# Sending six of eight head groups through the output projection with seven half-size products, summed by accumulating DMAs

## The chip, the cores and the metric

The kernel runs on one core of a Trainium2 chip. The metric is the device time in microseconds of one execution, here the median of three runs. All data are float32.

## The reference

One transformer block on `x` of 2 batches x 512 tokens x 512 features, with 32 heads of 128. Cut to what matters:

```python
q, k, v = rms_norm(n @ Wq + bq, gq), rms_norm(n @ Wk + bk, gk), n @ Wv + bv     # n = layernorm(x)
p = softmax(q_h @ k_h.T / sqrt(128))                                            # for each batch and head h
o_h = p @ v_h
attn = concat(o_h) @ Wo + bo                                                    # Wo: 4096 x 512
x = x + layernorm(attn)
x = x + layernorm(ffn(layernorm(x)))                                            # a linear layer and gated low-rank experts
```

## The kernel before, in words

The kernel does four stages one after the other: the projection to q, the projection to k, the attention loop (with the values' projection woven in), and the tail (residual, feed-forward, output).

**Projections.** `project` (L174) goes over 8 groups of 4 heads. It already uses a seven-product form: with batches as one pair and feature halves as the other, seven products of half size and some sums replace eight products. The sums of weights are made by GpSimd (`weight_sums` L163, `value_sums` L287), those of tokens by VectorE (`token_sums` L150). q, k and v are kept in DRAM and fetched again in the loop (`fetch`, `fetch_v`).

**The attention loop (L533)** has 64 iterations `i`, one per head and batch (`h, b = divmod(i, 2)`); eight iterations are one group `g` of 4 heads. The engines' order is that of the program (`IN_ORDER`: TensorE, VectorE, ScalarE, GpSimd; SyncE's DMA queue, SP, is not in that set). In iteration `i`:

- VectorE: `sums(i-1)` (L459 `quarters`, L467 `part`: the softmax's denominators), `below_top(i)` (L484, subtracts the maximum), after psd `inv`, `r` and `divided(i-1)` (L475 to L502), `top_of(i+1)` (L450, L451 `m`), then exits of value products and the addition `y` (L515).
- TensorE: `scores(i+1)` (L440 `pss`), a short matmul `psd` (L473), value products (L384 `v`), one output-projection task `psy` (L514), `weighted(i)` (L496 `o`).
- ScalarE: the scores' exits (L441), the exponential (L487), the value bias (L503).
- GpSimd: one partition maximum (L453 `top`), for which `below_top` of the next iteration waits.

**The output projection.** In group `g`'s iterations the tasks `outward(g-1, n)`, n from 0 to 7, run, one per iteration. Each has 4 matmuls: for one tile of 128 tokens, the group's four heads times their 128 x 512 rows of Wo, into one bank of PSUM. VectorE then adds the bank to the running sum `ys[n]` in SBUF. The eighth group's tasks come after the loop.

**Values.** 28 of their 112 tile steps come before the loop, 28 in its first 8 iterations, the rest until iteration 43. From iteration 44 on the loop has no value products.

**Buffers.** PSUM has two sets of 4 banks: `ps` for scores and psd, `aux` for the values, psy and o. A float32 matmul of the program is two records in the trace.

## Time and profile before

| | |
|---|---|
| median of 3 runs | 1365.17 us (1364.51 to 1367.77) |
| the profiled execution's own time | 1363.96 us |
| its span, first to last instruction | 1362.2 us |
| mean granted TensorE clock | 0.988 |
| DMA | 214.75 MB, mean 158 GB/s |

How to read the profile: PE is TensorE's matmul, PEld its weight load, DVE is VectorE, ACT ScalarE, POOL GpSimd, SPq the queue from which SyncE issues DMAs. A group row has line, engine, operation, output<-input, shapes and count, then busy time and the mean of one in ns, then the idle time just before and what ended it. In a row of windows stand the stretch, its length, the busy time of PE, PEld, DVE, ACT and POOL with the number of records in brackets, the granted clock, the DMA share and GB/s. A row of the timeline or of the chain has start, duration (us), engine and line.

```profile
POOL 3478888565763011111111111111111111111000
PEclk9999999999998999999999999999999999999988
DMA  6486665599999865532343252352343131300101
```

These are three of the rows with 40 equal slices of the span in tenths: GpSimd's busy share, the granted clock, the DMA engines' busy share. GpSimd is busy in the q and k projections (the first 12 or so slices), and little in the loop.

### The profile page before, as it was taken

Reading aid. Unit: us, or ns where it says so; the run is one execution under the profiler, and the core shown is the slowest. Engines: PE = TensorE matmul, PEld = TensorE weight load, DVE = VectorE, ACT = ScalarE, POOL = GpSimd, SP = SyncE. Lnnn points to the kernel's source line nnn. Section 1 sums busy time; section 2 is a strip of 40 time slices with the busy share of each in tenths; the row PEclk is TensorE's granted clock in tenths of the full one; section 3 lists DMA queues with packets and bytes.
Section 4 is the critical chain, followed back from the end, with each engine's and each line's share of the span. In section 5 each row is a group of like instructions: output and inputs, shape, how many; then the busy total and the mean of one; then the engine's idle time right before and its main releaser. Section 6 shows DMA issues by size and latency. Waiting matters only on the chain.

```text
span 1362.2 us, 10840 instructions
## 1 busy us (share of the span) xinstructions
PE 1319.9 (97%) x3244; PEld 599.4 (44%) x3244; DVE 926.2 (68%) x1206; ACT 488.0 (36%) x655; POOL 400.9 (29%) x294
## 2 busy tenths in 40 slices
PE   4999999999999999999999999999999999999976
PEld 2444444444444444444444444444444444444443
DVE  6443434777754478877777777777677888888566
ACT  4123232222131153443434334343433455444333
POOL 3478888565763011111111111111111111111000
PEclk9999999999998999999999999999999999999988
DMA  6486665599999865532343252352343131300101
GB/s 218 170 282 220 219 221 201 178 314 337 320 323 311 262 208 161 177 132 85 123 155 103 91 188 62 99 171 91 108 147 101 62 123 55 116 31 24 55 0 62
DMA packets 115083, 214.75 MB, mean 158 GB/s; under 512 B 10192, under 2 KB 10832, under 8 KB 115024
## 3 DMA queue, kind: packets, MB, share of 16 engines
q1 hardware_dynamic: 115024, 214.05, 47.0%
q8 instruction: 26, 0.43, 0.1%
q14 instruction: 33, 0.27, 0.1%
HBM read 136.42 MB, written 77.59 MB: 157 GB/s over the span
## 4 chain that ended last, share of the span: by engine, by line
PE 68%; DVE 2%; DMA 1%; ACT 0%; issue 0%; ACTq 0%
PE pss L440 16%; PE o L496 16%; PE psy L514 16%; PE v L384 14%; PE f L626 2%; PE p_k L192 2%; PE f L676 1%; PE psd L473 1%; PE hg L618 1%; DMA w_v<-keptw 1%; PE nt_f L139 0%; DVE st_z L123 0%; DVE quarters L459 0%; DVE s L484 0%; DVE z L600 0%; ACT s L487 0%
## 5 line engine op out<-in xcount | busy, mean ns | idle before, releaser
L441 ACT ACTIVATE s<-pss,rk 128x512 f32<-128x512 f32 x256 | 175.9, 687 | 464.6 <-PE pss L440 457.8
L453 POOL PARTITION_ALL_REDUCE top<-m x64 | 114.1, 1783 | 717.1 <-DVE m L451 717.1
L514 PE MATMUL psy<-wo,oh 128*128 128x512 f32 x512 | 230.8, 596 | 0.0
L496 PE MATMUL o<-s,v 128*128 128x512 f32 x512 | 230.3, 592 | 0.3 <-ACT s L487 0.3
L440 PE MATMUL pss<-qh,kh 128*128 128x512 f32 x512 | 230.2, 592 | 0.0
L496 PEld LDWEIGHTS o<-s,v 128*128 128x128 f32 x512 | 97.2, 190 | 123.1 <-issue 121.5
L440 PEld LDWEIGHTS pss<-qh,kh 128*128 128x128 f32 x512 | 97.3, 190 | 122.5 <-issue 122.5
L459 DVE TRANSPOSE_TENSOR_REDUCE quarters<-s 128x64 f32<-128x2048 f32 x64 | 147.3, 2301 | 0.0
L484 DVE TENSOR_TENSOR s<-s,top 128x2048 f32<-128x2048 f32 x64 | 146.0, 2281 | 0.0
L514 PEld LDWEIGHTS psy<-wo,oh 128*128 128x128 f32 x512 | 95.7, 190 | 112.4 <-issue 111.9
L487 ACT ACTIVATE s<-s 128x2048 f32<-128x2048 f32 x64 | 121.7, 1901 | 6.1 <-DVE s L484 6.1
L384 PE MATMUL v<-w_v,t 128*128 128x512 f32 x256 | 120.0, 613 | 3.3 <-DMA w_v<-keptw 3.3
L213 POOL TENSOR_TENSOR accq<-accq,sq_q 128x512 f32<-128x512 f32 x62 | 78.6, 1268 | 55.6 <-ACT sq_q L212 54.5
L213 POOL TENSOR_TENSOR acck<-acck,sq_k 128x512 f32<-128x512 f32 x62 | 85.4, 1382 | 24.7 <-ACT sq_k L212 21.7
L192 PE MATMUL p_q<-t,s_q 128*128 128x512 f32 x192 | 87.8, 607 | 2.6 <-DVE t L158 2.6
L384 PE MATMUL v<-w_v,nT_a 128*128 128x512 f32 x192 | 88.3, 601 | 0.0
L212 ACT ACTIVATE sq_k<-k 128x512 f32<-128x512 f32 x62 | 38.7, 630 | 137.8 <-DVE k L244 67.8
L212 ACT ACTIVATE sq_q<-q 128x512 f32<-128x512 f32 x62 | 39.1, 631 | 133.8 <-DVE q L244 78.2
L192 PE MATMUL p_k<-t,s_k 128*128 128x512 f32 x192 | 85.0, 592 | 0.0
L475 DVE RECIPROCAL inv<-psd 128x16 f32<-128x16 f32 x64 | 16.5, 257 | 99.6 <-PE psd L473 99.6
L450 DVE TENSOR_TENSOR m<-s 128x1024 f32<-128x1024 f32 x64 | 77.8, 1216 | 4.7 <-ACT s L441 4.7
L515 DVE TENSOR_TENSOR y<-psy,y 128x512 f32<-128x512 f32 x56 | 38.4, 691 | 57.6 <-PE psy L514 57.6
(152 smaller groups left out, 1418.5 us busy)
## 6 DMA issues: line engine op xcount, KB each, us to landing
keptq<-q SPq DMA_DIRECT2D x64, 256.0 KB, 4.0
q<-keptq SPq DMA_DIRECT2D x16, 1024.0 KB, 6.5
w_v<-keptw SPq DMA_DIRECT2D x32, 512.0 KB, 4.0
keptk<-k SPq DMA_DIRECT2D x64, 256.0 KB, 6.9
keptqs<-q SPq DMA_DIRECT2D x64, 256.0 KB, 6.9
qh<-keptqs SPq DMA_DIRECT2D x64, 256.0 KB, 2.9
kh<-keptk SPq DMA_DIRECT2D x64, 256.0 KB, 2.7
keptv<-o_v SPq DMA_DIRECT2D x64, 256.0 KB, 3.4
```

What stands on the lines that cost most here:

```text
L192: nc.tensor.matmul(ps, a[:, c, ts(j, P)], x[c], start=(c == 0), stop=(c == 1))
L212: nc.scalar.activation(sq, o, AF.Square)
L213: nc.gpsimd.tensor_tensor(accs[b], accs[b], sq, ALU.add)
L384: nc.tensor.matmul(ps, x[c][:, ts(t, P)], w[:, c, :], start=(c == 0), stop=(c == 1))
L440: nc.tensor.matmul(ps, kk[i][:, ts(k, P)], qs[i], start=True, stop=True)
L441: nc.scalar.activation(s[:, k, :], ps, AF.Copy, scale=rks[b][:, k : k + 1])
L453: nc.gpsimd.partition_all_reduce(ms[i], m[:, 0, :], P, ReduceOp.max)
L459: nc.vector.tensor_reduce(quarters.rearrange("p k j -> p (k j)"), ss[i].rearrange("p k (j r) -> p (k j) r", r=32), AX.X, ALU.add, apply_tr ...
L484: nc.vector.tensor_tensor(s, s, top.unsqueeze(1).to_broadcast([P, NT, 512]), ALU.subtract)
L487: nc.scalar.activation(ss[i], ss[i], AF.Exp)
L496: nc.tensor.matmul(po, vs[b, g, k][:, ts(j, P)], ss[i][:, k, :], start=(k == 0), stop=(k == NT - 1))
L514: nc.tensor.matmul(ps, o[:, ts(t, P)], wos[g][:, j, :], start=(j == 0), stop=(j == GH - 1))
```

## The change

The output projection of groups 0 to 5 is done by seven products. The left side is the heads' outputs, seen as 2 x 2 blocks: batch by even or odd pair member of the heads. The right side is Wo's rows for those heads by the two halves (256 columns) of the output.

- In the q stage SP loads the Wo rows of a group, VectorE makes four sums in place (`output_sums`), SP stores them in DRAM (`keptwo`).
- In every fourth iteration (`n4 == 0`) VectorE makes four sums of heads' outputs (`head_sums`) after `top_of`.
- `through_wo` is one task: a product `i`, a token half `u`, 4 matmuls of 256 columns into one bank. 14 tasks per group are spread over 8 iterations: 2, 2, 2, 1, 2, 2, 2, 1. The right sides are loaded by `load_right`, two products to a tile, at n = 7, 2 and 4.
- The result of a task goes to one of 14 running sums `acc`. For group 0 it is written there directly (VectorE with the bias for products 1 and 5, else ScalarE). For groups 1 to 5 ScalarE copies the bank into SBUF and GpSimd issues a DMA that adds the copy to the running sum.
- When iteration 56 is reached, VectorE makes the output's tiles from the running sums (`combined`, 14 operations, three per iteration). Groups 6 and 7 go the old way: group 6 in the last eight iterations, with each addition held back by an iteration, group 7 after the loop.
- Buffers are regrouped: x and value tiles in larger tiles, 16 `o` tiles for 13, a new pool `gpool`; the last Wo groups come into `hpool` by halves; the running sums take the weights' pool and six `y` tiles.

```diff
...
-    xpool = ctx.enter_context(tc.tile_pool(name="xpool", bufs=B * NT))
+    xpool = ctx.enter_context(tc.tile_pool(name="xpool", bufs=B * NT // 2))
-    ypool = ctx.enter_context(tc.tile_pool(name="ypool", bufs=B * NT))
+    ypool = ctx.enter_context(tc.tile_pool(name="ypool", bufs=6))
-    vpool = ctx.enter_context(tc.tile_pool(name="vpool", bufs=3 * NT))
+    vpool = ctx.enter_context(tc.tile_pool(name="vpool", bufs=4))
-    opool = ctx.enter_context(tc.tile_pool(name="opool", bufs=GH * B + 5))
+    opool = ctx.enter_context(tc.tile_pool(name="opool", bufs=16))
+    gpool = ctx.enter_context(tc.tile_pool(name="gpool", bufs=2))
-        xt = xpool.tile([P, D], F32, tag="x", name=f"{name}{b}_{t}")
+        halves = [xpool.tile([P, 2, D], F32, tag="x", name=f"{name}{b}_{u}") for u in range(NT // 2)]
...
-        out = [vpool.tile([P, 2, 256], F32, tag="v", name=f"s{i + 1}_{name}") for i in range(4)]
-        s1, s2, s3, s4 = out
+        pairs = [vpool.tile([P, 4, 256], F32, tag="v", name=f"s{i}_{name}") for i in range(2)]
+        s1, s2, s3, s4 = out = [t[:, i : i + 2] for t in pairs for i in (0, 2)]
...
+        WG = NG - 2
+        keptwo = dram.tile([WG, 2, P, 2, 512], F32, tag="wo", name="keptwo")
+        woq = wo.rearrange("(g j k p) f -> g k p j f", j=2, k=2, p=P)
+        wo_halves = {}
+        def load_halves(g):
+            pool, tag = ((hpool, "h"), (gpool, "g"))[g % 2]
+            wo_halves[g] = [pool.tile([P, 2, 512], F32, tag=tag, name=f"wo{g}_{k}") for k in range(2)]
+            for k in range(2):
+                nc.sync.dma_start(out=wo_halves[g][k], in_=woq[g, k])
+        def output_sums(g):
+            of = wo_halves[g]
+            (b11, b12), (b21, b22) = ([w[:, :, ts(e, 256)] for e in range(2)] for w in of)
+            nc.vector.tensor_tensor(b11, b12, b11, ALU.subtract)
+            nc.vector.tensor_tensor(b12, b22, b12, ALU.subtract)
+            nc.vector.tensor_tensor(b22, b22, b11, ALU.subtract)
+            nc.vector.tensor_tensor(b21, b22, b21, ALU.subtract)
+            for k in range(2):
+                nc.sync.dma_start(out=keptwo[g, k], in_=of[k])
...
             value_sums(g // 2, g % 2)
+            if 0 < g <= WG:
+                output_sums(g - 1)
+            if g < WG:
+                load_halves(g)
...
-            wos[g] = load_w(wo[ts(g, GH * P), :], f"wo{g}")
+            wos[g] = []
+            for k in range(2):
+                w = hpool.tile([P, 2, 512], F32, tag="h", name=f"wo{g}_{k}")
+                nc.sync.dma_start(out=w, in_=wo[ts(2 * g + k, 2 * P), :].rearrange("(j p) f -> p j f", p=P))
+                wos[g] += [w[:, j, :] for j in range(2)]
...
-        def fetch_v(b, g):
-            for t in range(NT):
-                v = vpool.tile([P, 512], F32, tag="v", name=f"v{b}_{g}_{t}")
-                nc.sync.dma_start(out=v, in_=keptv[b, g, t])
-                vs[b, g, t] = v
+        def fetch_v(b, c):
+            v = vpool.tile([P, NT, 256], F32, tag="v", name=f"v{b}_{c}")
+            src = keptv[b, c // 2].rearrange("t p f -> p t f")
+            nc.sync.dma_start(out=v, in_=src[:, :, ts(c % 2, 256)])
+            vs[b, c] = v
...
+            if (b, h % 2) != (1, 0):
+                left_of[{(0, 0): 1, (0, 1): 2, (1, 1): 4}[b, h % 2], h // 2] = o
+        two_halves = [wpool.tile([P, 4, 512], F32, tag="w", name=f"acc{n}") for n in range(2)]
+        accs = [t[:, n, :] for t in two_halves for n in range(4)]
+        accs += [ypool.tile([P, 512], F32, tag="y", name=f"acc_y{n}") for n in range(6)]
+        accs = [a.rearrange("p (t e) -> p t e", t=2) for a in accs]
+        acc = {i + 1: accs[2 * i : 2 * i + 2] for i in range(7)}
+        right_of = {}
+        def head_sums(c):
+            def tile_of(i):
+                return opool.tile([P, 512], F32, tag="o", name=f"s{i}_o{c}")
+            a11, a12, a21, a22 = (os[b, 2 * c + k] for b in range(B) for k in range(2))
+            s3, s2, s4 = tile_of(3), tile_of(2), tile_of(4)
+            nc.vector.tensor_tensor(s3, a11, a21, ALU.subtract)
+            nc.vector.tensor_tensor(a21, a21, a22, ALU.add)
+            nc.vector.tensor_tensor(s2, a21, a11, ALU.subtract)
+            nc.vector.tensor_tensor(s4, a12, s2, ALU.subtract)
+            left_of.update({(3, c): s4, (5, c): a21, (6, c): s2, (7, c): s3})
+        product_order = (1, 2, 4, 5, 7, 6, 3)
+        def load_right(g, n):
+            w = gpool.tile([P, 2, 512], F32, tag="g", name=f"wr{g}_{n}")
+            for half, i in enumerate(product_order[2 * n : 2 * n + 2]):
+                k, e = {1: (0, 0), 2: (1, 0), 3: (1, 1), 4: (1, 0), 5: (0, 0), 6: (1, 1), 7: (0, 1)}[i]
+                src = (woq if i <= 3 else keptwo)[g, k]
+                nc.sync.dma_start(out=w[:, half, :].rearrange("p (j f) -> p j f", j=2), in_=src[:, :, ts(e, 256)])
+                right_of[i, g] = w[:, half, :].rearrange("p (j f) -> p j f", j=2)
+        def through_wo(g, i, u):
+            ps = pt(f"psw{i}_{g}_{u}", "aux").rearrange("p (t e) -> p t e", t=2)
+            for t in range(2):
+                for j in range(2):
+                    a = left_of[i, 2 * g + j][:, ts(2 * u + t, P)]
+                    nc.tensor.matmul(ps[:, t, :], a, right_of[i, g][:, j, :], start=(j == 0), stop=(j == 1))
+            to = acc[i][u]
+            def add():
+                if g > 0:
+                    new = upool.tile([P, 512], F32, tag="u", name=f"w{i}_{g}_{u}").rearrange("p (t e) -> p t e", t=2)
+                    nc.scalar.copy(new, ps)
+                    nc.gpsimd.dma_start(out=to, in_=new, accum_op=ALU.add)
+                elif i in bias_of:
+                    nc.vector.tensor_tensor(to, ps, bias_of[i].unsqueeze(1).to_broadcast([P, 2, 256]), ALU.add)
+                else:
+                    nc.scalar.copy(to, ps)
+            return add
+        bias_of = {1: bo_b[:, 0:256], 5: bo_b[:, 256:512]}
+        nc.vector.tensor_tensor(bias_of[5], bias_of[5], bias_of[1], ALU.subtract)
+        y_pairs = {}
+        def combined(u):
+            for b in range(B):
+                y_pairs[b, u] = xpool.tile([P, 2, 512], F32, tag="x", name=f"y{b}_{u}")
+            a1, a2, a3, a4, a5, a6, a7 = (acc[i + 1][u] for i in range(7))
+            (c11, c12), (c21, c22) = ([y_pairs[b, u][:, :, ts(e, 256)] for e in range(2)] for b in range(B))
+            for out, p, q, op in (
+                (c11, a1, a2, ALU.add),
+                (a6, a1, a6, ALU.add),
+                (a7, a6, a7, ALU.add),
+                (a6, a6, a5, ALU.add),
+                (c12, a6, a3, ALU.add),
+                (c21, a7, a4, ALU.subtract),
+                (c22, a7, a5, ALU.add),
+            ):
+                yield lambda out=out, p=p, q=q, op=op: nc.vector.tensor_tensor(out, p, q, op)
+        def y_tile(b, t):
+            return y_pairs[b, t // 2][:, t % 2, :]
+        def outward(g, b, t, tag=None):
             ps = pt(f"psy{b}_{g}_{t}", tag or "aux")
             for j in range(GH):
                 o = os[b, g * GH + j]
-                nc.tensor.matmul(ps, o[:, ts(t, P)], wos[g][:, j, :], start=(j == 0), stop=(j == GH - 1))
-            return lambda: nc.vector.tensor_tensor(ys[n], ps, bo_b if g == 0 else ys[n], ALU.add)
-
+                nc.tensor.matmul(ps, o[:, ts(t, P)], wos[g][j], start=(j == 0), stop=(j == GH - 1))
+            return lambda: nc.vector.tensor_tensor(y_tile(b, t), ps, y_tile(b, t), ALU.add)
+        wo_tasks = {i: [] for i in range(N)}
+        for g in range(WG):
+            for k in range(14):
+                wo_tasks[G * (g + 1) + k * G // 14].append(
+                    lambda g=g, k=k: through_wo(g, product_order[k // 2], k % 2)
+                )
+        last = N - G
+        for b, t, n in [(b, t, n) for n, (b, t) in enumerate((b, 2 * u + t) for u in range(2) for b in range(B) for t in range(2))]:
+            wo_tasks[last + n].append(lambda b=b, t=t: outward(WG, b, t))
...
         for i in range(N):
             g, n = divmod(i, G)
             if i + 3 < N:
                 fetch(i + 3)
-            if n == 2:
+            c, n4 = divmod(i, 2 * B)
+            if 2 <= n4 and 0 < c < H // 2 - 1:
+                fetch_v(n4 - 2, c + 1)
+            if g >= WG and n == 6:
                 load_wo(g)
-            if n >= G - 2 and g + 1 < NG:
-                fetch_v(n - G + 2, g + 1)
+            if g < WG and n == 7:
+                for k in range(2):
+                    load_right(g, k)
+            if 0 < g <= WG and n in (2, 4):
+                load_right(g - 1, 1 + n // 2)
+            if n == 0 and g > WG:
+                combining = [step for u in range(2) for step in combined(u)]
             part = sums(i - 1) if i > 0 else None
             below_top(i)
             if i + 1 < N:
@@ -550,29 +680,38 @@
             while left and 84 - left < want:
                 exits.append(next(v_steps))
                 left -= 1
-            adds = [outward(g - 1, n)] if g > 0 else []
+            adds = [task() for task in wo_tasks[i]]
             top_of(i + 1)
+            if n4 == 0 and 0 < c <= 2 * WG:
+                head_sums(c - 1)
+            for _ in range(3):
+                if combining:
+                    combining.pop(0)()
+            if i >= last:
+                held, adds = adds, held
             for work in exits + adds:
                 work()
             po = weighted(i)
+        for add in held:
+            add()
...
-        adds = [outward(NG - 1, n, "ps") for n in range(NT)]
+        adds = [outward(NG - 1, 0, t, "ps") for t in range(NT)]
         for add in adds:
             add()
-        adds = [outward(NG - 1, NT + n, "aux") for n in range(NT)]
+        adds = [outward(NG - 1, 1, t, "aux") for t in range(NT)]
         for b in range(B):
-            x2 = ys[b * NT : (b + 1) * NT]
+            x2 = [y_tile(b, t) for t in range(NT)]
...
```

## The prediction

> **What bounds the kernel now.** I read the page first, then the windows by stage, one iteration of the attention loop in the timeline, the chain of waits, and the rows nearest to the new instructions. Engines on the page:
>
> ```profile
> PE 1319.9 (97%) x3244; PEld 599.4 (44%) x3244; DVE 926.2 (68%) x1206; ACT 488.0 (36%) x655; POOL 400.9 (29%) x294
> ```
>
> TensorE is busy 97% of the span. By stage (Q projection; K projection; loop with values still to do; loop without), TensorE's busy time stands first after the stretch, VectorE's third:
>
> ```profile
> 30.00:235.00 205.00, 202.06 (x470) 89.68 (x469) 84.67 (x126) 53.72 (x84) 154.69 (x124) 0.98 0.64 218
> 235.00:420.00 185.00, 184.41 (x431) 81.48 (x430) 136.30 (x174) 47.05 (x77) 115.31 (x85) 1.00 0.84 288
> 583.00:1058.00 475.00, 475.00 (x1162) 214.80 (x1161) 352.36 (x381) 189.42 (x224) 64.16 (x36) 1.00 0.36 117
> 1058.00:1265.00 207.00, 206.73 (x512) 93.66 (x511) 173.38 (x178) 100.50 (x116) 33.87 (x19) 1.00 0.22 71
> ```
>
> In the loop nothing makes TensorE wait: what leaves its stream leaves the kernel's time, if VectorE, 84% busy in the last stretch, keeps up. One iteration there, from the timeline (in brackets the idle time before and what ended it):
>
> ```profile
> 1181.08 2.30 DVE L459 TRANSPOSE_TENSOR_REDUCE quarters<-s 128x64 f32<-128x2048 f32 x1
> ...
> 1183.60 2.28 DVE L484 TENSOR_TENSOR s<-s,top 128x2048 f32<-128x2048 f32 x1
> ...
> 1187.14 0.29 PE L473 MATMUL psd<-part,same 128*128 128x16 f32 x2
> ...
> 1187.47 0.26 DVE L475 RECIPROCAL inv<-psd 128x16 f32<-128x16 f32 x1 [1.59 <-PE psd L473]
> ...
> 1190.37 0.69 DVE L451 TENSOR_TENSOR m<-m 128x512 f32<-128x512 f32 x1
> ...
> 1191.22 1.78 POOL L453 PARTITION_ALL_REDUCE top<-m  x1 [8.74 <-DVE m L451]
> ```
>
> The next quarters starts at 1191.61, so the period is 10.53 us. VectorE's reserve is the 1.59 us in which it waits for psd; GpSimd is idle 8.74 us.
>
> **TensorE, the gain.** The chain has a Wo task, and the narrowest matmuls with a new weight each, as:
>
> ```profile
> 1187.43 3.53 PE psy L514 x8
> ...
> 1328.91 3.76 PE hg L618 x32
> ```
>
> Each program matmul is two records. Eight in a row take 3.43 us behind a full-width matmul, 429 ns a record of 512 columns (3.53 directly behind the short psd; that 0.1 stays in both kernels). hg has 137 columns and takes 3.76 / 32 = 117.5 ns. On the line between, 256 columns take 117.5 + 119 x 311.5 / 375 = 216 ns. A group of four heads now costs 8 tasks x 3.43 = 27.44 us. Seven products x 2 token halves x 4 matmuls x 2 records = 112 records x 216 = 24.2 us. Six groups: 6 x 3.24 = **19.4 us gained**.
>
> A rule speaks against this. The Trainium skill, "TensorE: Matmul & The Clock Gate", Part 3, says that a weight load overlaps running matmuls only when its row group differs; all of ours use all rows. The LDWEIGHTS row says 190 ns, so by the rule a record costs 216 + 190 = 406 ns, a group 45.5 us, and six groups lose 108 us. The rows contradict it: hg's loads also take 189 ns each, yet its records come every 117.5 ns, so loads do overlap. I take 216; bounds 214.5 (half of 429) and 222.
>
> **VectorE.** Removed: 48 additions of psy at 0.69 us = 33 us. Added in the loop: 12 x 4 head sums like L451 (0.69 us, both inputs in SBUF) = 33 us; 14 combinations = 9.7 us; 4 bias additions = 2.8 us. The total barely moves; what counts is where it falls.
> - Head sums come four at once (about 2.5 us at their pitch) in every fourth iteration. Count from psd's end: m done +3.6, head sums +6.1, quarters and part +8.6, subtraction +10.9, exponential (1.9) done +13.0 with the hand-over. The next weighted matmul starts at +10.5 + 3.5 = +14.0. It fits by about 1 us. Over eight iterations TensorE needs 8 x 7.0 + 24.2 + 0.8 = 81 us, VectorE 8 x (8.94 - 0.61) + 5 = 72. Cost nothing; without this reserve the whole 2.5 us would show every fourth iteration.
> - The combinations add 3 x 0.62 in iterations 56 to 60, where psy additions remain: 8.94 + 1.9 = 10.8 against 10.53, five times, 1.4 us behind in all, nearly the 1.59 of reserve. Cost 0 to 1.5; I take **0.5**.
> - Where two value products fall in an iteration, five PSUM tiles pass through four "aux" banks. The first value exit, after m and head sums, is done at +6.1 + 0.7 = +6.8; weighted wants its bank at about +7.0. Nine iterations, half of them with two values, 0 to 0.5 us each: **0.5**.
> - Six times four output sums in the Q stage, 24 x 0.69 = 17 us. VectorE idles 4.46 us at each group boundary there, which takes 2.8. GpSimd adds then too: the K stage has GpSimd's addition at 1382 ns against 1268 in Q, and VectorE's two-input scaling at 1047 against 751 for the same operation from PSUM. At that price the four take 4.2, still under 4.46. TensorE leads. Cost 0, bound 3.
>
> **ScalarE.** 80 copies (70 later, 10 of the first group) x 0.58 (L397) = 46 us; per iteration 5.4 + 1.2 of 10.1 us. A copy stands ahead of the next scores' exit, which begins 4.9 us after its last work, so the idle time hides it. Cost 0.
>
> **GpSimd, the unknown.** 70 accumulating DMAs. No row shows a DMA issued there. The nearest is SP's: 0.3 to 0.4 us to issue, 2.0 to 4.5 to land for 256 KB. An accumulation also reads its target, so I estimate up to twice that landing; the sum is wanted 8 iterations later, or at the end at least one. For the issue the Trainium skill, "DMA: Bandwidth & Descriptors", Specifications, gives about 1 us to the first byte from GpSimd, which builds descriptors in software. I take 1 us: two per iteration plus 1.8 for the reduction is 3.8 of 10. Behind a waiting DMA stands only the next partition reduction, for which the subtraction on VectorE waits. The copies end near +8 and that reduction starts at +14, so 6 us are free: **0** below 3 us per DMA.
>
> **SP and DMA.** Q stage: 12.6 MB more (1 MB in, 1 MB out per group) over 144 us, 218 + 87 = 305 GB/s; the K stage ran at 288 with TensorE busy 184.4 of 185. Loop: weights 11 MB for 6.3, accumulation 18 MB, on a 0.22 to 0.36 share: hidden. SP has about six more issues per group. load_right waits for a tile that this iteration's Wo products release; behind it stand value stores, and key and query loads three iterations ahead: hidden. SP's queue isn't held in program order, so this is less sure. One load is late: the second half of the last Wo group goes into three buffers of which two are held until iteration 63, so it starts near that psy's end (1261.3 now) and takes 3.9 us; its matmuls start at 1265.3 + 1.7. It fits by 1.8 us unless SP is behind: 0 to 3, I take **1**. Buffer regrouping (x, v, o tiles): the new sets cover the lives I count (16 o tiles, at most 15 or 16 live): 0.
>
> **Sum.** -19.4 + 0.5 + 0.5 + 1 = -17.4 on the profiled execution's 1363.96 (span 1362.2): 1346.6. The median of the runs shown is 1365.17, 1.2 above it: **1348 us**, 1.3% faster. About 0.3%, 4 us, is what a measurement of this kernel can tell from no change.
>
> **Rivals.**
> - *As summed* (0.64): 1344 to 1352.
> - *Half of it is given back* (0.14): VectorE reaches the bound. If each of 12 head-sum bursts costs 0.7 us more than counted, 8 us go: 1356; range 1352 to 1361. For it: 1.59 us of reserve. Against it: the +13.0 against +14.0 above.
> - *Nothing to be seen* (0.07): 1361 to 1369. Reserved for queue waits of SP, or for products narrower but no shorter (245 ns a record gives no gain). Against it: hg.
> - *Slower, GpSimd bound* (0.13). The Trainium skill, "GPSIMD Engine Reference", section 2.1, says that the first call to a freshly loaded GpSimd kernel pays about 6 us. If alternating between reduction and DMA reloads code, or building is slow, eight iterations need 14d + 15.6 us for a price d per DMA. The loop with values has 102 us for eight (13.2 each, less 0.4), the one without 81: GpSimd binds the latter from d = 4.7, the former from 6.2. Over 28 and 12 iterations the loss is 70d - 400, which equals the gain at d = 6.0; at d = 6.5 it is 55, and the kernel takes 1348 + 55 = 1403 us. For it: nothing in the trace measures d. Against: the first reduction after 62 additions on GpSimd took 1.80 us and started 0.14 us after its input, so no reload stood between these two kinds.
> - *Better* (0.02): under 1344, 214.5 ns and no cost at all.
>
> **How the numbers follow.** Faster by over 0.3%: 0.64 + 0.14 + 0.02 = 0.80; within: 0.07; slower: 0.13. From 1343 to 1366 lie 0.64 + 0.14 + 0.02 and half of the third, 0.84.
>
> **What the profile would show.** Right: psw matmuls of 256 columns near 216 ns a record, TensorE's busy time about 19 us less, its idle time in the loop still near 0, GpSimd's DMA issues near 1 us and reductions still ending before VectorE asks. Wrong: weighted or psd waiting for VectorE in every fourth iteration (second case); the subtraction L484's successor waiting for top, or GpSimd busy 80% (slower); Q-stage matmuls waiting for DMA or VectorE; psy of the last group waiting for its weights.

## The result and the profile after

The changed kernel takes 1351.29 us (median of 4 runs, 1349.74 to 1357.32) against 1365.36 for the kernel before in the same session: a ratio of 0.9906, 95% interval 0.9884 to 0.9928. The profiled execution took 1352.03 us, with a span of 1350.3 (1362.2 before) at a granted clock of 0.991 (0.988). So 11.9 us went from the span where the prediction's sum had 17.4; the median lies 3.3 us above the 1348 predicted, 0.7 us inside the end of its range.

The page after, its line of engines, and from its windows the stretch of the loop without values (time in the window, then busy time of PE, PEld, DVE, ACT and POOL, granted clock, DMA share, GB/s):

```profile
PE 1300.9 (96%) x3532; PEld 652.3 (48%) x3532; DVE 978.9 (72%) x1249; ACT 533.6 (40%) x735; POOL 473.0 (35%) x364
```

```profile
1050.00:1253.00 203.00, 199.66 (x567) 103.39 (x566) 181.18 (x185) 108.14 (x133) 53.46 (x40) 1.00 0.42 106
```

TensorE lost 19.0 us of work (1319.9 to 1300.9), as predicted. But its idle time rose from 42.3 to 49.4 us. Before, it was busy 206.73 of 207 us in this stretch; now it misses 3.3 of 203, and VectorE is busy 89% of it.

Four groups that are new in the changed kernel (line, engine, operation, count | busy us, mean ns | idle time before it and what ended it):

```profile
L580 PE MATMUL psw<-wr,oh 128*128 128x256 f32 x384 | 88.3, 380 | 0.0
L586 ACT COPY w<-psw 128x512 f32<-128x512 f32 x70 | 40.6, 583 | 66.7 <-PE psw L580 51.5 <-issue 11.7 <-DVE o_v L425 1.9
L587 POOL DMA_DIRECT2D acc<-w x40 | 36.9, 972 | 13.7 <-ACT w L586 13.7
L558 DVE TENSOR_TENSOR oh<-oh,oh 128x512 f32<-128x512 f32 x12 | 16.1, 1340 | 1.3
```

The 380 ns are the length of overlapping records; two tasks (16 records) take 3.46 us by the timeline, 216 ns a record. An accumulating DMA occupies GpSimd for 0.97 us. L558, the second of the four head sums, takes 1340 ns where its neighbours take 0.69 us.

Where the time went, by the interval from one iteration's psd to the next (us; iterations 1 to 63, all others within 0.03 of their ideal):

| iteration | before | after | ideal | lost | what is late |
|---|---|---|---|---|---|
| 16, 24, 40 (with four head sums and two value products) | 13.96 each | 15.06, 15.71, 15.11 | 13.98 | 3.9 | weighted, for its PSUM bank |
| 45, 49 | 10.52 | 10.89, 10.62 | 10.54 | 0.4 | VectorE, in the iteration behind head sums |
| 47, 51, 55 (one Wo task, no value) | 10.52 | 9.71 each | 8.82 | 2.7 | weighted, for the exponential |
| 58 to 61 (combinations) | 10.52 each | 11.22, 11.58, 11.08, 10.86 | 10.53 | 2.6 | VectorE |

"Ideal" is TensorE's own work: two tasks 0.02 more than a psy task, one task 1.7 less. The losses come to 9.7 us before rounding, of which the prediction had 2. From the first Wo product to the experts' first product (hg) the loop took 708.55 us before and 698.46 after: 10.1 gained. In these two profiles the span's 11.9 us are this and 6.4 at the start of the values (below), less 2.1 before the first Q product, 1.2 in the Q stage and 1.2 in the K stage.

Iteration 24 in the timeline of the changed kernel (start, duration, engine, line; in brackets the idle time before it and what ended it):

```profile
791.69 3.62 PE L580 MATMUL psw<-wr,oh 128*128 128x256 f32 x16
792.13 2.07 POOL L487 PARTITION_ALL_REDUCE top<-m  x1 [7.97 <-DVE m L485]
792.66 1.34 DVE L558 TENSOR_TENSOR oh<-oh,oh 128x512 f32<-128x512 f32 x1
...
795.37 0.68 DVE L425 TENSOR_TENSOR o_v<-v,u_v 128x512 f32<-128x512 f32 x1
795.97 0.68 DVE L443 TENSOR_TENSOR u_v<-v,u_v 128x512 f32<-128x512 f32 x1
796.13 0.58 ACT L586 COPY w<-psw 128x512 f32<-128x512 f32 x1 [1.93 <-DVE o_v L425]
...
796.79 3.67 PE L530 MATMUL o<-s,v 128*128 128x512 f32 x8 [1.49 <-ACT w L586]
```

Weighted waits 1.49 us for a PSUM bank. Two releases come just before it: VectorE's addition L443, the second operation that reads the first value product, ends at 796.65, and ScalarE's second copy, which the bracket names, at 796.71. Which of them it waits for this trace can't tell; the experiment below that has no copies can, and it is VectorE. In iterations 16 and 40 the last such operation is the first value exit itself (the operation that empties the product's bank), which ends 7.7 us after psd's end; weighted begins 0.10 and 0.15 us later, after waits of 0.85 and 0.89 us. These operations stand behind the head sums, which take 3.5 us instead of the 2.5 counted, because one of them runs beside GpSimd's reduction. Iterations 20 and 36, also with head sums and two values, lose nothing: in 36 ScalarE empties the first value's bank; for 20 the traces don't say why.

Iteration 47, the same view:

```profile
1080.17 1.97 PE L580 MATMUL psw<-wr,s_o 128*128 128x256 f32 x8
1080.23 0.69 ACT L475 ACTIVATE s<-pss,rk 128x512 f32<-128x512 f32 x1 [0.17 <-PE pss L474]
...
1080.82 1.90 ACT L521 ACTIVATE s<-s 128x2048 f32<-128x2048 f32 x1
...
1082.77 3.70 PE L530 MATMUL o<-s,v 128*128 128x512 f32 x8 [0.63 <-ACT s L521]
```

With one Wo task TensorE has 1.97 us between psd and weighted. The exponential ends 2.7 us after psd's start, since it stands on ScalarE behind the copy of the fourth score tile. In the kernel before it ended as late, but there weighted came 3.66 us after psd's start:

```profile
1081.91 0.29 PE L473 MATMUL psd<-part,same 128*128 128x16 f32 x2
1082.69 1.90 ACT L487 ACTIVATE s<-s 128x2048 f32<-128x2048 f32 x1
1085.57 3.60 PE L496 MATMUL o<-s,v 128*128 128x512 f32 x8
```

So 1.0 us lay between the two, and a task that is 1.7 us shorter uses that up.

Iteration 58:

```profile
1199.02 2.08 POOL L487 PARTITION_ALL_REDUCE top<-m  x1 [9.38 <-DVE m L485]
1199.37 1.53 DVE L614 TENSOR_TENSOR y<-acc 128x512 f32<-128x512 f32 x1
1200.82 0.68 DVE L614 TENSOR_TENSOR acc_y<-acc,acc_y 128x512 f32<-128x512 f32 x1
...
1204.76 0.36 PE L507 MATMUL psd<-part,same 128*128 128x16 f32 x2 [0.21 <-DVE part L501]
```

The second combination takes 1.53 us beside the reduction, the third 0.68 outside it. Now psd waits for VectorE.

Outside the loop the two profiles differ most at the start of the values. Before, TensorE waited there for the value weights (timeline, then windows with columns as above):

```profile
433.69 11.75 PE L384 MATMUL v<-w_v,t 128*128 128x512 f32 x20 [3.26 <-DMA w_v<-keptw]
```

```profile
430.00:435.00 5.00, 1.74 (x3) 0.82 (x3) 0.69 (x1) 0.00 (x0) 0.00 (x0) 0.78 1.03 372
435.00:440.00 5.00, 5.00 (x7) 1.89 (x7) 0.69 (x1) 0.00 (x0) 0.00 (x0) 0.54 0.86 278
440.00:445.00 5.00, 5.00 (x13) 2.24 (x12) 2.08 (x3) 0.00 (x0) 0.00 (x0) 1.00 0.53 182
```

The wait cost 3.26 us, and behind it the granted clock was 0.54 for 5 us: 7 records instead of 13. From the first value product to the first score product it was 40.8 us before and 34.4 after, 6.4 less, which no step of the prediction has. Two 1 MB Wo loads, issued at 415.69 and 417.82 ahead of those weights, are gone in the changed kernel. Whether they are the cause is a question for the experiments.

### The profile page after: what moved, and what is told of

Its sections match the earlier page's. It is cut to its first block, busy times and chain, and to the rows that moved or that the text cites. A ratio compares the mean times of both kernels' runs of the same rounds, so it can differ in the third digit from the quotient of the medians.

```text
span 1350.3 us, 11826 instructions
## 1 busy us (share of the span) xinstructions
PE 1300.9 (96%) x3532; PEld 652.3 (48%) x3532; DVE 978.9 (72%) x1249; ACT 533.6 (40%) x735; POOL 473.0 (35%) x364
## 4 chain that ended last, share of the span: by engine, by line
PE 62%; DVE 6%; ACT 1%; issue 1%; ACTq 0%; DVEq 0%
PE pss L474 15%; PE o L530 15%; PE v L417 15%; PE psw L580 10%; PE psy L624 2%; PE f L765 2%; PE p_k L194 2%; DVE quarters L493 1%; DVE s L518 1%; ACT s L521 1%; PE f L815 1%; DVE m L484 1%; PE hg L757 1%; DVE y L614 1%; PE psd L507 1%
## 5 line engine op out<-in xcount | busy, mean ns | idle before, releaser
L487 POOL PARTITION_ALL_REDUCE top<-m x64 | 119.0, 1860 | 615.8 <-DVE m L485 615.8
L521 ACT ACTIVATE s<-s 128x2048 f32<-128x2048 f32 x64 | 121.8, 1903 | 14.0 <-DVE s L518 12.8
L417 PE MATMUL v<-w_v,t 128*128 128x512 f32 x256 | 116.8, 600 | 0.0
L580 PE MATMUL psw<-wr,oh 128*128 128x256 f32 x384 | 88.3, 380 | 0.0
L580 PEld LDWEIGHTS psw<-wr,oh 128*128 128x128 f32 x384 | 72.5, 190 | 19.8 <-issue 11.5
L417 PEld LDWEIGHTS v<-w_v,t 128*128 128x128 f32 x256 | 46.7, 190 | 49.3 <-issue 49.0
```

The lines of the kernel that those rows point to most:

```text
L417: nc.tensor.matmul(ps, x[c][:, ts(t, P)], w[:, c, :], start=(c == 0), stop=(c == 1))
L487: nc.gpsimd.partition_all_reduce(ms[i], m[:, 0, :], P, ReduceOp.max)
L521: nc.scalar.activation(ss[i], ss[i], AF.Exp)
L580: nc.tensor.matmul(ps[:, t, :], a, right_of[i, g][:, j, :], start=(j == 0), stop=(j == 1))
```

## The experiments

Times are medians of the timed runs, "loop" is from the first Wo product to hg in the profile. The kernel before had medians of 1364.96 to 1365.5 us beside all of these runs.

**Late head sums.** They are emitted behind the value exits instead of ahead of them.

```
-            if n4 == 0 and 0 < c <= 2 * WG:
-                head_sums(c - 1)
...
-            for work in exits + adds:
+            for work in exits:
+                work()
+            if n4 == 0 and 0 < c <= 2 * WG:
+                head_sums(c - 1)
+            for work in adds:
```

> The changed kernel with the four head sums moved behind the exits of the value products on VectorE. Theory A (in iterations 16, 24 and 40 the weighted matmul waits 1.1, 1.7 and 1.1 us for a PSUM bank whose exit stands behind the head sums, directly or through a tile of the exits): the three iterations go back to 13.97 us, 3.9 us less in all, and nothing else moves. Theory B (these waits come from the accumulating DMAs or their copies, not from the head sums' place): the three stay above 15 us or others take their place.

Measured: 1347.93 us (ratio 0.9867, 0.9844 to 0.9889); loop 694.24. Iterations 16, 24 and 40 took 13.98 us, all others as in the changed kernel but 45 (10.62). Iteration 24 there:

```profile
788.58 1.78 POOL L487 PARTITION_ALL_REDUCE top<-m  x1 [7.96 <-DVE m L485]
...
791.50 0.69 DVE L558 TENSOR_TENSOR oh<-oh,oh 128x512 f32<-128x512 f32 x1
791.59 3.60 PE L530 MATMUL o<-s,v 128*128 128x512 f32 x8
```

Away from the reduction the sum takes 0.69 us and the reduction 1.78 rather than 2.07, and weighted waits for nothing. The place of the head sums cost 3.9 us. The other 0.3 of the loop is iteration 45. It takes 10.62 us also in two experiments below that leave the head sums alone. Where it takes 10.62, the exponential begins 1.68 us after psd's start, behind the subtraction. Where it takes 10.89, as in both profiles of the changed kernel, it begins at 1.95, behind the reciprocal that follows.

**VectorE adds instead of ScalarE and the DMAs.** The six later groups' products are added from PSUM.

```
-                    new = upool.tile([P, 512], F32, tag="u", ...)...
-                    nc.scalar.copy(new, ps)
-                    nc.gpsimd.dma_start(out=to, in_=new, accum_op=ALU.add)
+                    nc.vector.tensor_tensor(to, ps, to, ALU.add)
```

> The changed kernel without the copies and the accumulating DMAs: VectorE adds each of the 70 tasks' banks to its running sum, as it did with psy. Theory A (VectorE is the next bound, and the way over ScalarE and GpSimd is what keeps the additions off it): in the stretch with values nearly no change, 13 us period against 10 to 11 of VectorE work; in iterations 44 to 55 VectorE gets 21 additions of 0.62 more than its 8.3 to 9.0 us, 10.1 to 10.6 each against 10.1 of TensorE, so 3 to 8 us are lost there, and the kernel takes 3 to 10 us more. Theory B (the DMAs and the copies cost more than they hide): it is faster by 2 us or more.

Measured: 1355.23 us (ratio 0.9916, 0.9888 to 0.9943); loop 701.71, 3.25 more than in the changed kernel. Iteration 20 rose from 13.98 to 15.11, iterations 44 and 48 from 10.54 to 11.28, 45 and 49 to 11.08; elsewhere VectorE had room for the 70 additions. The way over ScalarE and GpSimd saves some 3 us, not more.

Iterations 16, 24 and 40 took as long as in the changed kernel, 15.06, 15.70 and 15.10 us. In iteration 24:

```profile
794.78 0.68 DVE L425 TENSOR_TENSOR o_v<-v,u_v 128x512 f32<-128x512 f32 x1
795.38 0.68 DVE L443 TENSOR_TENSOR u_v<-v,u_v 128x512 f32<-128x512 f32 x1
...
796.21 3.67 PE L530 MATMUL o<-s,v 128*128 128x512 f32 x8 [1.49 <-DVE u_v L443]
```

There is no copy on ScalarE here, the additions that replace it come only at 797.17, and weighted still waits 1.49 us and begins 0.15 us behind L443. So it is VectorE's last reading of the first value product that releases the bank, and the copy that the changed kernel's trace names only came at the same time.

**No accumulating DMAs.** The copies stay; the sums of groups 1 to 5 are left out of the output.

```
-                    nc.gpsimd.dma_start(out=to, in_=new, accum_op=ALU.add)
```

> The changed kernel without the 70 accumulating DMAs (groups 1 to 5 are then missing from the output projection of the six groups); the copies out of PSUM stay. Theory A (the DMAs are hidden: 0.97 us each on GpSimd, which is idle for 7 of 10 us, and 3.5 to 4.3 us to land on DMA engines with half their time free): the loop's iterations keep their lengths within 0.1 us, the kernel within 2 us of the changed one. Theory B (descriptor building or the DMAs' traffic slow VectorE, the reduction or the loads): the loop gets shorter by 3 us or more, and the reduction's and the head sums' longer rows (2.07 for 1.78, 1.34 for 0.69) return to the short ones.

Measured: 1349.97 us (ratio 0.9876, 0.9848 to 0.9905); loop 698.18 against 698.46. Every iteration but the 45th (10.62 for 10.89) took the same, and that one also takes 10.62 in the next experiment, where the DMAs stay. So the 70 DMAs cost the loop nothing that shows. Nor are they what lengthens the head sum and the reduction: L558 still takes 1340 ns and the reduction 1861 ns in the mean (1860 with the DMAs).

**The two Wo loads put back.** Into the changed kernel's running-sum tiles, whose content is overwritten later.

```
+        for n, t in enumerate(two_halves):
+            nc.sync.dma_start(out=t, in_=wo[ts(n, GH * P), :].rearrange("(c p) f -> p c f", p=P))
```

> The changed kernel with one thing put back: two loads of 1 MB of Wo each, as the kernel before had them, into the tiles of the running sums before these are first written (the data are overwritten, the output is unchanged). Theory A (the stage from the first value product to the first scores lost 6.4 us, 40.8 to 34.4, because the old kernel's first two Wo loads stood in the DMA queues ahead of the first stored value weights): the stage goes back to about 40 us, the wait of the value products for w_v returns with some 3 to 6 us, and the kernel takes about 6 us more than the changed kernel. Theory B (that stage differs between executions or because the DMA queue is ordered otherwise): the stage stays at 34 to 35 us and the time is unchanged.

Measured: 1353.87 us (ratio 0.9926, 0.9902 to 0.995), 2.6 over the changed kernel, with overlapping intervals. The value stretch stayed at 34.4 us, with no wait for w_v. But one appeared earlier, at the last K group:

```profile
397.75 4.60 PE L194 MATMUL p_k<-nT_a,w_k 128*128 128x512 f32 x5 [4.30 <-DVE q L347]
```

```profile
397.75 1.71 POOL L170 TENSOR_TENSOR s_k<-w_k 128x512 f32<-128x512 f32 x1 [11.48 <-DMA w_k<-in_wk]
```

The bracket names VectorE, but GpSimd's first sum of the same weights (L170) began at 397.75 too, ended by the landing of w_k, so w_k is what was late. These weights were issued at 387.94, the loads put back only at 413.84 and 420.32. They can't have caused that wait. So a theory that the two loads by themselves cost 6.4 us didn't hold.

**The kernel before, with those loads later.** A small write by GpSimd into their tiles keeps them out of the K stage.

```
         def load_wo(g):
-            wos[g] = load_w(wo[ts(g, GH * P), :], f"wo{g}")
+            w = wos[g] = wpool.tile([P, 4, 512], F32, tag="w", name=f"wo{g}")
+            if g < 2:
+                nc.gpsimd.memset(w[:, 0, 0:1], 0.0)
+            nc.sync.dma_start(out=w, in_=wo[ts(g, GH * P), :].rearrange("(c p) f -> p c f", p=P))
```

> This is the kernel before with one edit: its first two Wo loads (1 MB each) follow a small write by GpSimd into their tiles, so that they are no longer sent among the last loads of the K stage; the Wo products are not changed. Theory (those 2 MB stand ahead of the value weights on the DMA engines, so that TensorE waits 3.3 us for them, and the granted clock falls to 0.54 for the 5 us after): no wait for w_v, the stretch from the first value product to the first score product falls from 40.8 to 34 to 35 us, and the median from 1365 to about 1359. Rival (the DMA engines are behind at the end of the K stage with or without these loads, as the experiment that put the loads back into the changed kernel suggests, whose value stretch stayed at 34.4 while a wait of 4.3 us appeared at the last weights of the K stage): the wait moves to another place or stays, from the first K product to the first score product still 210 to 212 us, median 1364 to 1366.

Measured: 1362.51 us (ratio 0.9983, 0.997 to 0.9997). The value stretch was 34.4 us without a wait for w_v. The local part of the theory holds, its size doesn't: 0.4 to 4.1 us by the interval, 2.9 by the medians, not 6.

**Both kernels once more.**

> The changed kernel once more, for a second profile: nothing differs. If the wait for the last K weights is a matter of how the transfers of one run meet, the stretch from the first K product to the first value product, 172.0 us in the first profile and 171 to 179 in experiments that do not touch it, differs from 172.0 by up to 7 us, and the loop's iterations are the same to 0.1 us. If it is fixed by the program, it is 172.0 within 0.5.

> The kernel before once more, for a second profile: nothing differs. Theory that the two Wo loads cost the value stretch 6.4 us in every run: 40 to 41 us from the first value product to the first score product, with a wait of about 3 us for w_v. Rival, that the wait falls now at the last K weights, now at the value weights, as the transfers meet: 34.4 to 41, and if it is short, the K stretch (170.8 in the first profile) is longer.

Measured: 1352.26 us (ratio 0.9917, 0.989 to 0.9943) and 1365.66 (1.0003). The K stretch is counted from the ssq product, which stands behind the first K group. It took 172.7 us in the changed kernel (172.0 in its first profile) and 173.8 in the kernel before (170.8), whose value stretch was now 36.1 us, with waits of 1.94 at the last w_k and 1.47 at w_v. Loop and iterations repeated to 0.1 us. Over both stretches, from ssq to the first score product, the kernel before took 211.6 and 209.9 us; ten profiles with the changed kernel's loads took 205.8 to 213.6, 209.0 in the mean, with single waits for w_k of 1.2 to 5.5. The DMA engines are behind there in each run (shares over 1.0 in windows of 5 us), and which weights come late differs from run to run. Most of the 6.4 us was the luck of the first two profiles. The means differ by 1.8 us, less than the ten differ among themselves (standard deviation 2.8), so what belongs to the kernels rests on the experiment before this one: about 2 us, between 0.4 and 4.1.

**Exponential early in the three short iterations.** In 47, 51 and 55 it is emitted ahead of the fourth score tile's copy.

```
                 nc.tensor.matmul(ps, kk[i][:, ts(k, P)], qs[i], start=True, stop=True)
+                if k == NT - 1 and before_last:
+                    before_last()
...
-                scores(i + 1)
-            exponentials(i)
+                scores(i + 1, (lambda: exponentials(i)) if i in (47, 51, 55) else None)
+            if i not in (47, 51, 55):
+                exponentials(i)
```

> In iterations 47, 51 and 55 alone the exponential is put ahead of the copy of the fourth score tile on ScalarE; nothing else differs. Theory (these iterations, with one Wo task, are bound by ScalarE's order: the exponential stands behind the fourth copy, which waits for the fourth score product): 9.71 us each goes to about 9.0, 2 us in all. Rival (VectorE or the divisor chain bounds them at 9.7 anyway): 9.6 to 9.8, no gain. The head sums and combinations stay as they are, so iterations 16, 24, 40 and 58 to 61 keep their times.

Measured: 8.86, 8.85 and 8.85 us, loop 695.87 (2.6 less). There is one timed run only (1353.4 us), with a long K stage, so this rests on the profile's iterations; later experiments repeat them. The timeline of iteration 47 (code lines are two further down):

```profile
1083.64 1.90 ACT L523 ACTIVATE s<-s 128x2048 f32<-128x2048 f32 x1
...
1085.44 0.68 ACT L477 ACTIVATE s<-pss,rk 128x512 f32<-128x512 f32 x1
1085.66 3.63 PE L532 MATMUL o<-s,v 128*128 128x512 f32 x8
```

Weighted follows its Wo task with no wait. The order on ScalarE was the bound.

**Combinations on GpSimd.**

```
-                yield lambda ...: nc.vector.tensor_tensor(out, p, q, op)
+                yield lambda ...: nc.gpsimd.tensor_tensor(out, p, q, op)
```

> The 14 combining additions are done by GpSimd instead of VectorE; nothing else differs from the changed kernel. Theory (VectorE, with three combinations more per iteration, is late for the subtraction and so for the exponential): iterations 58 to 61, which took 11.22, 11.58, 11.08 and 10.86 us, come back to 10.5 to 10.6, so the part with Wo work is 2.7 us shorter. Rival (the delay is that of the last Wo group's tasks and weights, not of the combinations): they stay at 11 to 11.6. Second rival (GpSimd's additions, twice as long as VectorE's, now hold up the partition reductions): two or more of the iterations are over 11.6.

Measured: 1396.79 us in a single run, some 45 slower than the changed kernel; iterations 57, 60 and 61 took 28.0, 19.7 and 17.8 us. None of the theories had that. GpSimd's timeline around iteration 57:

```profile
1180.82 1.78 POOL L487 PARTITION_ALL_REDUCE top<-m  x1 [7.14 <-DVE m L485]
1189.68 1.88 POOL L614 TENSOR_TENSOR y<-acc 128x512 f32<-128x512 f32 x1 [7.08 <-issue]
...
1193.31 1.26 POOL L614 TENSOR_TENSOR acc_y<-acc_y,acc_y 128x512 f32<-128x512 f32 x1
1200.58 1.80 POOL L487 PARTITION_ALL_REDUCE top<-m  x1 [6.01 <-issue]
```

Between a reduction and an addition lie 7.1 us, between the addition and the next reduction 6.0, in which GpSimd waits for nothing the profile shows ("issue"). All the later changes between the two kinds, here and in the next experiment, are alike, 6.0 to 7.8 us. VectorE's maximum was ready at 1192.1, so the reduction came 8.5 us late, and with it the subtraction, the exponential and TensorE. Between two additions there is no such gap.

**Three edits at once.** The late head sums, the early exponential and the GpSimd combinations together, expected before the result of the last was known.

> The changed kernel with three edits together: head sums behind the value exits, combinations on GpSimd, the exponential ahead of the fourth score copy in iterations 47, 51 and 55. If the three losses are separate and add up (3.9 + 2.7 + 2 us), the median is 8 to 9 us under the changed kernel's 1351.3, about 1343, with iterations 16, 24 and 40 at 13.98, 58 to 61 at 10.5 and 47, 51, 55 at about 9. If one loss only covers another (GpSimd, which would then add, also delays the last reductions), the gain is 4 to 6 us, 1345 to 1347.

Measured: 1389.8 us (ratio 1.0165, 1.0139 to 1.019). The first two gains are there in the iterations (13.98, 8.86), under some 40 us of the third edit, now in five runs.

**Two combinations per iteration.** On VectorE again, with late head sums and the early exponential.

```
-            for _ in range(3):
+            for _ in range(3 if n == 0 else 2):
```

> The changed kernel with three edits: head sums behind the value exits, the exponential ahead of the fourth score copy in iterations 47, 51 and 55, and the combinations left on VectorE but two per iteration (three in the first) instead of three. Theory (VectorE is over its period by three combinations beside a Wo addition: 8.94 + 1.9 = 10.8 against 10.53, and under it by two: 10.2): iterations 58 to 61 fall from 11.22, 11.58, 11.08, 10.86 to about 10.55, and iterations 16, 24, 40, 47, 51, 55 are as in the experiments with one edit, so the part with Wo work is 9.1 us shorter than in the changed kernel, whose median was 1351.3: 1342 to 1344. Rival (something else delays iterations 58 to 61, for instance the last Wo group's loads): they stay over 11, 1345 to 1347.

Measured: 1345.76 us (ratio 0.9857, 0.9832 to 0.9882); loop 691.85. Iterations 58 to 62 took 10.52, 10.70, 10.85, 10.85 and 9.10: 52.0 us in sum against 51.8 with three per iteration. My theory failed; the delay only moved to the end. The second of the two still runs beside the reduction (from iteration 60, both combinations in the first row):

```profile
1214.42 2.13 DVE L616 TENSOR_TENSOR acc_y<-acc_y,acc_y 128x512 f32<-128x512 f32 x2
1214.67 2.08 POOL L489 PARTITION_ALL_REDUCE top<-m  x1 [8.78 <-DVE m L487]
```

VectorE is busy without a gap in iterations 60 and 61, 10.85 us each. Less the 0.84 us that the reduction adds, that would be 10.0, under the 10.53 of TensorE.

**Combinations where VectorE waits.** As the last, but they stand between the subtraction and the reciprocal.

```
+            for _ in range(3 if n == 0 else 2):
+                if combining:
+                    combining.pop(0)()
             if i > 0:
                 divided(i - 1, po, reciprocals(i - 1, part))
...
             top_of(i + 1)
-            for _ in range(3 if n == 0 else 2):
-                if combining:
-                    combining.pop(0)()
```

> The kernel with three edits of the run before, but the combinations, two per iteration (three in the first), stand between VectorE's subtraction and its reciprocal, where it waited 1.59 us for psd and GpSimd runs no reduction, instead of behind the maximum, where the second of them took 1.53 us beside the reduction. Theory (the price of a combination is its contention with the reduction, and the place beside it): all take 0.69, iterations 58 to 62 fall from 52.0 us in sum to 49.3 (4 x 10.53 + 7.1), the part with Wo work is 9.2 us shorter than the changed kernel's 698.5 (6.6 with the edits before), median 1342 to 1343. Rival (VectorE is over its period by its sum alone, wherever the additions stand): 51.5 to 52 us for these five, 1344 to 1346. Second rival (the reciprocal is now late for the quotient that the next Wo product reads): over 52.

Measured: 1344.82 us (ratio 0.9856, 0.9838 to 0.9873). Iterations 58 to 62 took 10.52, 10.52, 10.53, 10.52 and 7.09, 49.2 us; loop 689.01. VectorE and GpSimd in iteration 58:

```profile
1188.35 0.68 DVE L616 TENSOR_TENSOR y<-acc_y,acc 128x512 f32<-128x512 f32 x1
...
1188.95 0.68 DVE L616 TENSOR_TENSOR y<-acc_y,acc_y 128x512 f32<-128x512 f32 x1
...
1189.56 0.25 DVE L511 RECIPROCAL inv<-psd 128x16 f32<-128x16 f32 x1
...
1193.05 0.68 DVE L627 TENSOR_TENSOR y<-psy,y 128x512 f32<-128x512 f32 x1
1193.30 1.78 POOL L489 PARTITION_ALL_REDUCE top<-m  x1 [8.23 <-DVE m L487]
```

Both additions take 0.68 us, in the time in which VectorE waited for psd before. The iterations are as the theory had them; the median is 2 us above its 1342 to 1343, with a K stretch of 174.7 us in the profile against 172.0. This loop is 19.54 us shorter than that of the kernel before, and the kernel is the best of all tried, 6.5 us under the changed one.

## Why the prediction was right, and where not

- **TensorE, 19.4 us gained: right.** 216 ns a record as interpolated, 19.0 us less work on the page, and 19.54 of gain in the loop where the last experiment leaves almost nothing else in the way. The rule weighed there, that loads of all rows don't overlap, doesn't hold for these: 190 ns loads beside records every 216 ns.
- **Head sums, cost nothing, and the PSUM banks, 0.5: right in mechanism, wrong in size.** They are one cause and cost 3.9 us. The step that failed is "The first value exit ... is done at +6.1 + 0.7 = +6.8". It named the right bank, m was done at +3.6 and weighted wanted the bank at +7.0, as counted. But the sums took 3.5 us, not 2.5, as the second met the reduction, so the exit ended at +7.7. In iteration 24 a second operation of VectorE, which the step left out, reads the bank until +8.3. This is the rival "half of it is given back" in three iterations of 12.
- **ScalarE, cost nothing: wrong, 2.7 us.** The failed step looked only at what the new copies hold up. In an iteration with one task and no value product, TensorE reaches weighted 1.7 us sooner, and the exponential, behind the fourth score copy, becomes the bound. The 1.0 us that it had to spare stood in the trace of the kernel before. "Where a stall goes, what is late next" was not asked of the shorter iterations.
- **Combinations, 0.5: 2.6 us.** "8.94 + 1.9 = 10.8 ... five times, 1.4 us behind in all" priced each at 0.62. One of three ran beside the reduction at 1.53, 0.84 more, so the reserve of 1.59 was gone in two iterations. Moving them out of the reduction's time took the whole cost away; having fewer per iteration didn't. That move also put them where VectorE waits; the 10.0 us estimated above say that being apart from the reduction is enough.
- **GpSimd, 1 us per DMA and no cost: right** (0.97 us each, and no cost in the loop). The reason given against the slower rival was not sound, though: the first reduction after 62 additions came 0.14 us after its input because GpSimd had been idle for 40.5 us before it. The combinations put on GpSimd show 6.0 to 7.8 us for each change between additions and reductions. What kept the change clear of it is that issuing a DMA between reductions causes no such gap: the loop without DMAs is no faster.
- **The last Wo load, 1 us: 0.** From the last psd to hg both kernels take 31.25 us.
- **Q stage, 0: right.** From the first Q product to ssq 233.0 and 230.9 us in two profiles, 231.8 and 232.3 before, though two of the four output sums took 1641 ns, beside GpSimd's additions.
- **Not in the prediction:** about 2 us gained at the end of the K stage by the two Wo loads that went. In the sum: 19.5 less 9.5 in the loop, and 2 there, is 12, against 12.8 by the ratio (9.8 to 15.8).

That the median fell into the summed case's 1344 to 1352 is in part luck. The loop's 10.1 us alone lead to 1355, into the rival's range of 1352 to 1361. What brought it under 1352 are the gain at the K stage, which no step had, and the scatter of the K stage; the second measurement of the same kernel was 1352.26.

What remains open: why the waits for w_k differ between runs of one kernel, and why the exponential of iteration 45 is held until the reciprocal in some of these programs.

## What to carry to other kernels

When a change frees the engine that bounds, go through each iteration that gets shorter and ask which queue it now catches up with; a price from the mean iteration misses those. Price a two-input VectorE operation by what GpSimd runs at that moment, and put it where VectorE waits anyway. A buffer is free when its last reader has run, so find every reader and count what stands in front of it at its measured length. Where two releases come within 0.1 us, a run without one of them tells which counts, not the name in the bracket. And before a second kind of work goes to an engine, look for a trace in which the two kinds follow one another without idle time between.

## What the runs showed of the hardware

- GpSimd: 6.0 to 7.8 us of "issue" at each change between a partition reduction and an elementwise addition, in both directions; none between reductions with DMA issues among them, and none before a small memset straight behind a reduction (in the kernel before with the later loads). The Trainium skill, "GPSIMD Engine Reference", section 2.1, gives about 6 us for the first call to a freshly loaded kernel with no visible instruction. That fits, but that code was loaded anew at each change is not shown: the profile's two instruction queues carried 28 and 35 packets in that run, and 28 and 35 or 36 in the changed kernel.
- An addition on VectorE with both inputs in SBUF takes 1.34 to 1.68 us instead of 0.69 when a reduction or addition of GpSimd runs beside it, and the reduction 2.07 instead of 1.78. With one input in PSUM (y from psy, in the last experiment) it takes 0.68 beside the reduction's start, and the reduction 1.78. The Trainium skill, "SBUF — State Buffer", "Who interferes with whom", has the contention, as an exclusive lock in which the loser waits out the whole instruction. Here both lose a part: in iteration 58 the addition ended at 1200.90, 0.2 us before the reduction.
- At waits of TensorE between 390 and 440 us of these profiles the granted clock, in windows of 2 us, fell to 0.50 to 0.56, and stayed under 1.00 for 4 to 9 us in all, part of the wait included, where the wait was 1.94, 1.96 or from 2.7 to 5.5 us. After a wait of 2.49 us (the changed kernel once more), and one of 2.41 at 347 us (early exponential), it stayed at 1.00, as after all of 1.8 us and less. The Trainium skill, "TensorE: Matmul & The Clock Gate", Part 1, has a free-running window of about 3.4 us behind this, which would make the phase decide. But it asks for at least one whole idle window, and waits of 1.94 us are shorter than that.
